# A two-layer graph attention kernel: products that end bank by bank, and rows spread by DMA rather than by transposes

## The chip, the cores and the metric

The kernel runs on one core of a Trainium2 chip. The metric is the device time of one launch in microseconds (us), the median over several runs. Everything is computed in 32-bit floats, except masks, which are stored as 16-bit floats.

## The reference

Two attention layers over a graph of 2708 nodes with 1024 features. `adj` is a 0/1 matrix of 2708 x 2708.

```python
# layer 0
h = jnp.maximum(_layernorm(x, axis=-1), 0.0)
f = h @ Wf + bf;  g = h @ Wg + bg
scores = jnp.where(adj > 0, jax.nn.relu(f @ g.T), -9e15)
x = x + jax.nn.softmax(scores, axis=1) @ (h @ W + bW)
# layer 1
h = jnp.maximum(_layernorm(x, axis=-1), 0.0)
hW = h @ W1;  f1 = hW @ a1;  f2 = hW @ a2
scores = jnp.where(adj > 0, jax.nn.leaky_relu(f1 + f2.T, negative_slope=0.2), -9e15)
x = x + jax.nn.relu(jax.nn.softmax(scores, axis=1) @ hW)
```

Two facts of it matter here. In layer 1 a score is a sum of something per row and something per column, so that a whole tile of scores is made from a column of numbers (one per partition) and a row of numbers spread over all partitions. In layer 0 the scores get a similar row, `r`.

## The kernel before

The kernel works in panels of columns of the transposed attention matrix: five panels (`NP` = 5), 576, 576, 532, 512 and 512 wide, each of two halves of `h` columns (288, 288, 266, 256, 256). The 2708 nodes along the other side are 20 tiles of 128, taken as ten pairs (`NQ` = 10), and two leftovers of 128 and 20 rows. All large products use seven products of half-size matrices in place of eight (M1 to M7, of Strassen's kind), with sums and differences on VectorE (DVE).

For each panel p, layer 0 runs `project_q`, `scores(p)`, the softmax, `aggregate(0, p)`, which multiplies the panel of weights with the features, and later `project(0, p)` by the weight matrix. Layer 1 has no score product: `weights1` makes the panel of weights on ScalarE (ACT) and DVE, and `aggregate(1, p)` and `project(1, p)` follow. The weights of panel p + 1 are made while panel p is multiplied.

**The aggregate.** `aggregate` hands its products in the order M1, M5, M2, M6, M3, M7, M4 to `accumulate` (L554 to L585). Each product accumulates into four PSUM banks (d = 0 to 3), named `gx`, `gy`, `gz` or `gv`. With `by_k` the loop runs over the ten pairs k outside and the four banks inside. After the last pair come the leftovers (`left_over`, L822 to L832: four matmuls of 128 rows, four of 20 rows, loaded as `hl`), and only then four evictions, one per bank, on ACT or DVE:

```python
if by_k:
    if m in more:
        more[m](ps)
    for d in range(NH):
        evict[m](d, ps[d])
    behind(rate)
```

M2 and M3 and M4 have such leftovers; those of M7 go apart into four banks `gw` in its middle (`into_m15`) and are added by DVE to a tile (`m15`, shown in the profile as `m<-gw`) before M7 is evicted. `prepare` and `then` are hooks after a product: after M3 the sums of the weights (`inverse_sums`: `sum_ps` by TensorE, a reciprocal on DVE), after M7 the scaling of results on GpSimd (`scale`).

**Rows out of columns.** A vector that lies as columns (128 partitions x up to 5) becomes a row on all partitions with `spread` (L229 to L240): a TensorE transpose of the column, broadcast, into a bank `sp_ps`, and copies of the bank into the tile, one for each four columns, in turn by DVE and ACT. So are made `rb` from `r` at the start of `scores(p)`, and in `weights1` the rows `ub` (from the columns `z`) and `vb1` (from `none`, called m in the code). The columns are made by DVE in `take_shifts(p + 1)`, the hook after M3 of layer 1's aggregate; the rows in `take_weights(p + 1)`, the hook after M7. A unit of weights P then is one ACT operation on `vb1`, one DVE operation on `ub`, one DVE addition of a mask tile (`maskl`), and an exponential on ACT.

**What sets the order.** TensorE, DVE, ACT and GpSimd each execute their queue in a fixed order, which a scheduler works out from the program and its dependencies when the kernel is built. SyncE (SP) issues loads in the order of the program (`load`); GpSimd issues the stores (`store`). Vector work that may be done at leisure is put in a list (`put`) and taken from it by `behind(us)`, which `accumulate` calls after every third pair and at a product's end.

Of the kernel before, what the change touches and what calls it, by code (L numbers as in the profile page):

```python
# [8 lines left out]
FP = mybir.dt.float32  # L9
# [9 lines left out]
P = 128  # L19
W = 512  # L20
# [37 lines left out]
def kernel(  # L58
# [19 lines left out]
    nc = InOrder(tc)  # L78
    N, D = x.shape
    NC = D // P  # L80
    NH = NC // 2
# [3 lines left out]
    NP = N // W  # L85
# [3 lines left out]
    width = [W + NM, W + NM, W + NY, W, W]  # L89
    base = [sum(width[:p]) for p in range(NP)]  # L90
    F = W // P
    MONO, TINY = F * NP, F * NP + 1
# [67 lines left out]
    md_d = dram.tile([P, 7, NH, W], FP, name="md_d")  # L160
    wt_d = [dram.tile([P, 4, NH, W], FP, name=f"wt{l}_d") for l in range(2)]
    mk_d = [dram.tile([P, NQ + 1, 2, width[p]], BF, name=f"mk_d{p}") for p in range(NP)]
    x1_d = [dram.tile([P if t < TINY else NY, D], FP, name=f"x1_d{t}") for t in range(NT)]

    ident = consts.tile([P, P], FP, name="ident")
# [31 lines left out]
    def behind(us, psum_free=False):  # L197
        credit[0] = min(credit[0] + us, 2 * us)
        while later and credit[0] > 0 and (psum_free or not later[0][3]) and (not later[0][4] or later[0][4]()):
            credit[0] -= one()  # L200

    def flush():
        while later:
            one()
# [24 lines left out]
    def spread(o, cols):  # L229

        at = 0
        for g in range(0, len(cols), 4):
            ps = bank("sp_ps")
            w = 0
            for cl in cols[g:g + 4]:
                n = cl.shape[0]
                nc.tensor.transpose(ps[:, w:w + n], cl.to_broadcast([n, P]), ident[:n, :n])
                w += n
            copy(o[:, at:at + w], ps[:, :w])
            at += w  # L240

    def add(o, a, b):
        nc.vector.tensor_tensor(o, a, b, OP.add)
# [4 lines left out]
    def columns_of(p, col):  # L248
        return [col[:n, i:i + 1] for i, (_, n) in enumerate(pieces[p])]
# [301 lines left out]
        picks.append(t)  # L551


    def accumulate(left, right, K, h, order, then, evict, name, prepare={}, rate=0.0, by_k=False, more={}, room=()):  # L554

        acc = {}
        at = {M1: "x", M2: "x", M5: "y", M3: "y", M6: "z", M7: "z", M4: "v" if by_k else "z"}
        for m in order:  # L560
            start = at[m] not in acc
            if start:
                acc[at[m]] = [bank(f"{name}{at[m]}{d}") for d in range(NH)]
            ps = [t[:, :h] for t in acc[at[m]]]
            for k, d in ([(k, d) for k in range(K) for d in range(NH)] if by_k else
                         [(k, d) for d in range(NH) for k in range(K)]):
                nc.tensor.matmul(ps[d], left(m, k, d), right(m, k), start=(start and k == 0),  # L567
                                 stop=(k == K - 1 and m not in more), skip_group_check=True)
                if by_k and d == NH - 1 and k % 3 == 2:
                    behind(rate)  # L570
                if by_k and d == NH - 1 and k == K // 2 and (m, k) in more:
                    more[m, k]()
                if not by_k and k == K - 1:
                    evict[m](d, ps[d])
                    behind(rate, m in room)
            if by_k:
                if m in more:
                    more[m](ps)
                for d in range(NH):
                    evict[m](d, ps[d])  # L580
                behind(rate)
            if m in prepare:
                prepare[m]()
            if m in then:
                then[m]()  # L585
# [202 lines left out]
    def aggregate(l, p, S, sm, then={}, rate=3.0):  # L788


        w = width[p]
        h = w // 2
        lo, hi = slice(0, h), slice(h, w)
        T1 = [slot("T1", (P, 2, HX)) for _ in range((NQ + 1) // 2)]
        t1 = lambda q: T1[q // 2][:, q % 2, :h]
        wa_ = lambda q: S[pairs[q][0]]
        wb_ = lambda q: S[pairs[q][1]]
        exps_until(NQ)
        for q in range(NQ):
            sub(t1(q), wa_(q)[:, hi], wa_(q)[:, lo])  # L800

        def second():
            exps_until(2 * NQ + 2 + LAG)
            for q in range(NQ):
                sub(wa_(q)[:, hi], wb_(q)[:, hi], wa_(q)[:, hi])
            for q in range(NQ):
                sub(wa_(q)[:, lo], wb_(q)[:, hi], t1(q))

        def fourth():
            for q in range(NQ):  # L810
                sub(wb_(q)[:, lo], wb_(q)[:, lo], wa_(q)[:, lo])

        hc = {}

        def left(m, q, d):
            i, j = group_of[q]
            if (m, i) not in hc:
                hc[m, i] = stream("hc", (P, 2, W))
                load(hc[m, i], hg_d[l][i][:, m])
            return hc[m, i][:, j, d * P:(d + 1) * P]  # L820

        def left_over(ps, e, s, start=False):  # L822


            two = stream("hl", (P, W + P))
            load(two, hgl_d[l][:, e])
            for d in range(NH):
                nc.tensor.matmul(ps[d], two[:, d * P:(d + 1) * P], S[MONO][:, s], start=start, stop=False,
                                 skip_group_check=True)
            for d in range(NH):  # L830
                g = slice(B32 * d, B32 * d + NY)
                nc.tensor.matmul(ps[d], two[g, W:], S[TINY][g, s], start=False, stop=True, skip_group_check=True)  # L832

        def into_m15():
            ps = [bank(f"gw{d}")[:, :h] for d in range(NH)]
            left_over(ps, 1, hi, True)
            for d in range(NH):
                add(get("m15", d), ps[d], get("m15", d))

        def right(m, q):  # L840
            if m == M5:
                return t1(q)
            s = wa_(q) if m in (M1, M6, M7) else wb_(q)
            return s[:, hi if m in (M3, M7) else lo]

        G = [None, None]
        tmp = {}
        part = lambda t, d: t[d // 2][:, d % 2, :h]

        def g(e, d, s):  # L850
            if G[0] is None:
                G[:] = both("gT")
            return G[e].rearrange("p (c i) -> p c i", c=NH)[:, d, s]

        def get(name, d):
            if name not in tmp:
                tmp[name] = in_pairs(name)
            return part(tmp[name], d)

        evict = {M1: lambda d, ps: nc.scalar.copy(get("m1", d), ps),  # L860
                 M5: lambda d, ps: add(get("m15", d), ps, get("m1", d)),
                 M2: lambda d, ps: nc.scalar.copy(g(0, d, lo), ps),
                 M6: lambda d, ps: add(get("u2", d), ps, get("m1", d)),
                 M3: lambda d, ps: add(g(0, d, hi), ps, get("u2", d)),
                 M7: lambda d, ps: (add(g(1, d, hi), ps, get("m15", d)), add(get("m1", d), ps, get("m1", d))),
                 M4: lambda d, ps: add(g(1, d, lo), ps, get("m1", d))}
        inverse = []
        of = lambda e, s: G[e].rearrange("p (c i) -> p c i", c=NH)[:, :, s]
        by = lambda s, k: inverse[0][:, s].rearrange("p (o i) -> p o i", o=1).to_broadcast([P, NH, k])

        def scale():
            for e, s, k in ((0, slice(0, w), w), (1, hi, h)):
                nc.gpsimd.tensor_tensor(of(e, s), of(e, s), by(s, k), OP.mult)  # L873

        accumulate(left, right, NQ, h, (M1, M5, M2, M6, M3, M7, M4), then, evict, "g",
                   {M5: second, M2: fourth, M3: lambda: inverse.append(inverse_sums(p, sm)), M7: scale}, rate=rate,
                   by_k=True, more={M2: lambda ps: left_over(ps, 0, lo), M3: lambda ps: left_over(ps, 0, hi),
                                    M4: lambda ps: left_over(ps, 1, lo), (M7, NQ // 2): into_m15})
        nc.vector.tensor_tensor(of(1, lo), of(1, lo), by(lo, h), OP.mult)
        return [t.rearrange("p (c i) -> p c i", c=NH) for t in G]  # L880
# [148 lines left out]
    def spread_wa():  # L1029
        for k in range(2):  # L1030
            spread(wab[k], [wa[:, k, c:c + 1] for c in range(NC)])
# [23 lines left out]
    def scores(p, B):  # L1055
# [3 lines left out]
        lo, hi = slice(0, h), slice(h, w)  # L1059
        fetch, convert, turn = makers[p]  # L1060
        rb = slot("rb")
        spread(rb, columns_of(p, r_[:, first_col[p]:]))
        acc = slot("acc")
        S = [None] * NT
        rates = (0.6, 1.0, 0.65, 0.65, 0.65)
# [36 lines left out]
        for q in range(NQ):  # L1102
            n = P
# [256 lines left out]
    for p in range(NP):  # L1360
# [17 lines left out]
        G[p] = aggregate(0, p, S, got["sm"], then)  # L1378
        if p == 0:
            flush()  # L1380
            spread_wa()
        if p < NP - 2:
            project(0, p, G.pop(p), finish0(p), {M1: lambda p=p: first_masks(p + 1, 0),
# [6 lines left out]
    def weights1(p, z, m, shift):  # L1390
# [2 lines left out]
        ub, vb1, sm = slot("ub"), slot("vb1"), slot("sm")  # L1393

        def spreads():
            spread(ub, columns_of(p, z))
            spread(vb1, columns_of(p, m))
        if p == 0:
# [67 lines left out]
    def take_shifts(p):  # L1466
        flush()
        got["zm"] = shifts1(p)

    def take_weights(p):  # L1470
        got["P"] = weights1(p, *got["zm"])
# [38 lines left out]
```

## Time and profile before

| | before |
|---|---|
| time, median of 3 | 3137.77 us (3136.57 to 3138.36) |
| profiled span | 3134.0 us |
| TensorE busy | 3046.8 us, 97%, 12712 instructions |
| DVE busy | 1827.0 us, 58% |
| ACT busy | 447.2 us, 14% |
| GpSimd busy | 464.3 us, 15% |
| granted TensorE clock, mean | 0.991 |
| DMA | 651.82 MB, 208 GB/s |

A 32-bit matmul is two instructions here, so the counts of TensorE are larger than the number of calls in the code. "Busy" counts the time in which an engine has an instruction under way; "waits" list the idle time of an engine by what ended it. The costliest groups of instructions are the matmuls of `aggregate` (L567), each product some 185 us in all, and those of the scores (L1077).

### The profile page before, as it was taken

To read this page: it belongs to the slowest core of one execution; us is meant where nothing else is said; L and a number is where in the kernel's file an instruction comes from. 1 tells how busy PE (TensorE), PEld (TensorE's weight loads), DVE (VectorE), ACT (ScalarE), POOL (GpSimd) and SP (SyncE) were. 2 spreads that over 40 slices of the span, in tenths; PEclk is the share of its full clock that TensorE was granted. 3 is DMA by queue.
4 is the path that set the end of the run, shared out by engine and by line. 5 is a ranking of instruction groups with operands and counts; after the bars stand their busy time and mean duration, and the time that the engine had idled before them with its cause. 6 is when DMAs were issued, how large, how long until landed. Compare 5 with 4: busy or idle time off the path is not lost.

```text
span 3134.0 us, 36230 instructions
## 1 busy us (share of the span) xinstructions
PE 3046.8 (97%) x12712; PEld 2261.3 (72%) x12712; DVE 1827.0 (58%) x3730; ACT 447.2 (14%) x788; POOL 464.3 (15%) x668
## 2 busy tenths in 40 slices
PE   8988999999999999999999999998999999999998
PEld 4566777667877588876888885865757758678684
DVE  5867686286732687327872478659483561745612
ACT  3321020000200102000020002103040130311200
POOL 2643002210002110023000101021010020120202
PEclk9989999999999999999999999998999999999999
DMA  6889838878446796477955678596665565565655
GB/s 219 307 284 280 258 122 311 231 228 253 147 134 159 220 258 205 147 175 240 294 167 154 169 220 243 192 300 234 194 186 168 160 197 162 164 197 171 216 163 190
DMA packets 379109, 651.82 MB, mean 208 GB/s; under 512 B 170848, under 2 KB 211328, under 8 KB 378928
## 3 DMA queue, kind: packets, MB, share of 16 engines
q1 hardware_dynamic: 335920, 525.38, 55.7%
q0 software_dynamic: 43008, 124.13, 11.9%
q8 instruction: 101, 1.65, 0.2%
q14 instruction: 80, 0.66, 0.1%
HBM read 536.68 MB, written 112.67 MB: 207 GB/s over the span
## 4 chain that ended last, share of the span: by engine, by line
PE 83%; DVE 5%; DMA 4%; issue 4%; POOL 2%; SPq 1%; ACT 0%; POOLq 0%; DVEq 0%; ACTq 0%
PE gy L567 12%; PE gz L567 12%; PE gx L567 11%; PE sz L1077 7%; PE gv L567 5%; PE pz L969 5%; PE sx L1077 5%; PE sy L1077 4%; PE px L969 4%; PE py L969 4%; PE qz L567 3%; PE qy L567 2%; PE qx L567 2%; SPq L139 1%; PE M_ps L483 1%
## 5 line engine op out<-in xcount | busy, mean ns | idle before, releaser
L1077 PE MATMUL sz<-B,As 128*128 128x288 f32 (+2 forms) x1200 | 292.7, 393 | 8.2 <-DVE st L45 7.5
L1077 PEld LDWEIGHTS sz<-B,As 128*128 128x128 f32 x1200 | 227.6, 190 | 58.3 <-DVE st L45 11.9
L873 POOL TENSOR_TENSOR gT<-gT,rr 128x2304 f32<-128x2304 f32 (+5 forms) x20 | 72.7, 3634 | 1101.0 <-DVE rr L45 998.6
L1077 PE MATMUL sx<-B,As 128*128 128x288 f32 (+2 forms) x800 | 201.5, 395 | 12.6 <-DMA As<-hs_d 11.7
L1077 PE MATMUL sy<-B,As 128*128 128x288 f32 (+2 forms) x800 | 199.0, 392 | 0.0
L567 PE MATMUL gz<-P,hc 128*128 128x288 f32 (+2 forms) x800 | 186.0, 393 | 2.3 <-ACT gT L45 2.3
L567 PE MATMUL gz<-Sa,hc 128*128 128x288 f32 (+2 forms) x800 | 186.0, 393 | 2.3 <-ACT gT L45 2.3
L567 PE MATMUL gx<-P,hc 128*128 128x288 f32 (+2 forms) x800 | 185.3, 393 | 0.1
L1077 PEld LDWEIGHTS sx<-B,As 128*128 128x128 f32 x800 | 152.3, 191 | 44.4 <-DMA As<-hs_d 12.2
L567 PE MATMUL gy<-T,hc 128*128 128x288 f32 (+2 forms) x800 | 184.2, 391 | 0.0
L567 PEld LDWEIGHTS gz<-Sa,hc 128*128 128x128 f32 x800 | 151.2, 190 | 36.0 <-ACT gT L45 4.4
L567 PEld LDWEIGHTS gz<-P,hc 128*128 128x128 f32 x800 | 150.9, 190 | 35.7 <-ACT gT L45 4.5
L567 PEld LDWEIGHTS gx<-P,hc 128*128 128x128 f32 x800 | 152.6, 191 | 32.7 <-issue 1.9
L567 PEld LDWEIGHTS gy<-T,hc 128*128 128x128 f32 x800 | 152.0, 190 | 30.5
L1077 PEld LDWEIGHTS sy<-B,As 128*128 128x128 f32 x800 | 151.7, 190 | 30.6 <-DVE st L45 0.3
L969 PE MATMUL pz<-w,ps 128*128 128x512 f32 x320 | 142.1, 594 | 0.8 <-DVE pt L45 0.8
L969 PE MATMUL py<-w,ps 128*128 128x512 f32 x320 | 142.1, 593 | 0.0
L969 PE MATMUL px<-w,gT 128*128 128x512 f32 x320 | 141.8, 595 | 0.0
L143 POOL DMA_DIRECT2D out_dram<-x_res x180 | 88.9, 500 | 265.3 <-DVE x_res L45 241.1
L45 DVE TENSOR_TENSOR gT<-gy,u 128x288 f32<-128x288 f32 (+2 forms) x40 | 14.8, 433 | 183.5 <-PE gy L832 183.5
L45 DVE TENSOR_TENSOR u<-gz,m 128x288 f32<-128x288 f32 (+2 forms) x40 | 17.6, 440 | 170.4 <-PE gz L567 169.9
L143 POOL DMA_DIRECT2D mk_d<-mask x55 | 35.9, 653 | 544.1 <-DVE mask L45 509.5
(318 smaller groups left out, 5089.8 us busy)
## 6 DMA issues: line engine op xcount, KB each, us to landing
hc<-hg_d SPq DMA_DIRECT2D x350, 512.0 KB, 3.9
As<-hs_d SPq DMA_DIRECT2D x150, 512.0 KB, 5.4
w<-wt_d SPq DMA_DIRECT2D x96, 512.0 KB, 5.2
w<-in_L_gnn_W_dram SPq DMA_DIRECT2D x72, 512.0 KB, 4.4
md<-md_d SPq DMA_DIRECT2D x56, 512.0 KB, 4.8
adj_i<-in_adj_dram SPq DMA_DIRECT2D x200, 128.0 KB, 5.0
hs_d<-hsT POOLq DMA_DIRECT2D x40, 512.0 KB, 5.0
hg_d<-g POOLq DMA_DIRECT2D x36, 512.0 KB, 5.1
```

Of the source, the lines that this page charges most:

```text
L45: i = f(*a, **k)
L139: tc.keep_in_program_order(nc.sync.dma_start(a, b))
L143: nc.gpsimd.dma_start(a, b)
L483: nc.tensor.matmul(ps, wfT[a][c // NH][:, c % NH, :], wgT[b][c], start=(c == 0), stop=(c == NC - 1))
L567: nc.tensor.matmul(ps[d], left(m, k, d), right(m, k), start=(start and k == 0), stop=(k == K - 1 and m not in more), skip_group_check=True)
L873: nc.gpsimd.tensor_tensor(of(e, s), of(e, s), by(s, k), OP.mult)
L969: nc.tensor.matmul(ps, left[i][m][:, k, :], w_[k], start=(start and k == 0), stop=(k == NH - 1), skip_group_check=True)
L1077: nc.tensor.matmul(ps[:n, :h], lefts[q][:, i % 2, c, :n], B[m][c // 2][:, c % 2, :h], start=(start and c == 0), stop=(c == NH - 1), skip_g ...
```

## The change

There are three parts. First, the products of the aggregate end bank by bank: eight of the ten pairs run as before, then the leftover products, and then for each bank the last two pairs, after which the bank is evicted at once. This lets the evictions overlap the product's own last matmuls. Second, the rows `r` of panels 1 to 4 are written to DRAM once by GpSimd and loaded back, spread over all partitions, by SyncE at the start of `scores(p)`. Third, the columns `z` and `none` of layer 1's panels 1 to 4 are written to DRAM by GpSimd in `take_shifts` as soon as they are ready, and loaded back as `ub` and `vb1` by two DMAs on GpSimd's queue. Both are meant to take the transposes and copies of `spread` from TensorE, DVE and ACT. Panel 0 keeps `spread` in both.

```diff
+    r_d = [dram.tile([1, WX], FP, name=f"r_d{p}") for p in range(NP)]
+    uv_d = [[dram.tile([1, WX], FP, name=f"uv{k}_d{p}") for k in range(2)] for p in range(NP)]
...
+    def columns_to_row(row, p, col):
+
+        k = len(pieces[p])
+        nc.gpsimd.dma_start(row[0:1, :W].rearrange("o (i p) -> p (o i)", p=P), col[:, :F])
+        if k > F:
+            n = pieces[p][F][1]
+            nc.gpsimd.dma_start(row[0:1, W:W + n].rearrange("o n -> n o"), col[:n, F:k])
+
+    def row_on_all(o, row, p, by=load):
+        by(o[:, :width[p]], row[0:1, :width[p]].to_broadcast([P, width[p]]))
...
+    TAIL = 2
...
-            for k, d in ([(k, d) for k in range(K) for d in range(NH)] if by_k else
-                         [(k, d) for d in range(NH) for k in range(K)]):
-                nc.tensor.matmul(ps[d], left(m, k, d), right(m, k), start=(start and k == 0),
-                                 stop=(k == K - 1 and m not in more), skip_group_check=True)
-                if by_k and d == NH - 1 and k % 3 == 2:
+            whole = K - TAIL
+            for k, d in ([(k, d) for k in range(whole) for d in range(NH)] + [(k, d) for d in range(NH) for k in range(whole, K)]
+                         if by_k else [(k, d) for d in range(NH) for k in range(K)]):
+                nc.tensor.matmul(ps[d], left(m, k, d), right(m, k), start=(start and k == 0), stop=(k == K - 1),
+                                 skip_group_check=True)
+                if by_k and d == NH - 1 and k < whole and (k % 3 == 2 or k == whole - 1):
                     behind(rate)
                 if by_k and d == NH - 1 and k == K // 2 and (m, k) in more:
                     more[m, k]()
-                if not by_k and k == K - 1:
+                if by_k and d == NH - 1 and k == whole - 1 and m in more:
+                    more[m](ps)
+                if k == K - 1:
                     evict[m](d, ps[d])
-                    behind(rate, m in room)
+                    if not by_k:
+                        behind(rate, m in room)
             if by_k:
-                if m in more:
-                    more[m](ps)
-                for d in range(NH):
-                    evict[m](d, ps[d])
                 behind(rate)
...
         rb = slot("rb")
-        spread(rb, columns_of(p, r_[:, first_col[p]:]))
+        if p == 0:
+            spread(rb, columns_of(p, r_[:, first_col[p]:]))
+        else:
+            row_on_all(rb, r_d[p], p)
...
             flush()
+            for s in range(1, NP):
+                columns_to_row(r_d[s], s, r_[:, first_col[s]:])
...
         def spreads():
+            if p > 0:
+                for o, row in zip((ub, vb1), uv_d[p]):
+                    row_on_all(o, row, p, nc.gpsimd.dma_start)
+                return
             spread(ub, columns_of(p, z))
             spread(vb1, columns_of(p, m))
...
     def take_shifts(p):
         flush()
         got["zm"] = shifts1(p)
+        for row, col in zip(uv_d[p], got["zm"]):
+            columns_to_row(row, p, col)
```

More of the change, by code (lines that the diff above doesn't have):

```diff
@@ L831, in left_over @@
                 g = slice(B32 * d, B32 * d + NY)
-                nc.tensor.matmul(ps[d], two[g, W:], S[TINY][g, s], start=False, stop=True, skip_group_check=True)
+                nc.tensor.matmul(ps[d], two[g, W:], S[TINY][g, s], start=False, stop=start, skip_group_check=True)
         def into_m15():
```

## The prediction

> **What bounds the kernel now.** I read the page's busy times first, then the chain of waits, then TensorE's waits by releaser, and last the timeline around those waits that the change touches.
>
> ```profile
> PE 3046.8 (97%) x12712; PEld 2261.3 (72%) x12712; DVE 1827.0 (58%) x3730; ACT 447.2 (14%) x788; POOL 464.3 (15%) x668
> PEclk9989999999999999999999999998999999999999
> ```
>
> TensorE (PE) is busy 97% of the span at nearly full clock; no other engine is near. Its chain share, 83%, says the same. So only two things pay: fewer TensorE instructions, or fewer gaps between them. DVE, ACT and GpSimd (POOL) time counts only where TensorE waits for it. The waits of TensorE in the kernel before (total us, times, longest):
>
> ```profile
> PE sx L1077 <- DMA As<-hs_d: 11.7, 1, 11.7
> PE sz L1077 <- DVE st L45: 7.5, 9, 1.4
> PE sum_ps L771 <- DVE gT L45: 5.1, 10, 0.5
> PE gz L567 <- ACT gT L45: 4.6, 10, 0.5
> PE sp_ps L237 <- DVE m L45: 3.8, 1, 3.8
> PE gx L567 <- DMA hc<-hg_d: 3.2, 1, 3.2
> PE gx L828 <- DMA hl<-hgl_d: 2.0, 1, 2.0
> ```
>
> The `sum_ps` and `gz` rows are ten waits each, one per panel and layer: in `aggregate`, after M2 the first matmul of M6, and after M3 the column sums, stand behind the evictions of a product that has just ended. The timeline of layer 1, panel 2 around the end of M3 and M7 (start us, us, engine and instruction, in brackets the idle time before it and its releaser):
>
> ```profile
> 2454.98 0.77 PE L832 MATMUL gy<-P,hl 20*128 20x288 f32 x8
> 2455.76 1.55 DVE L45 TENSOR_TENSOR gT<-gy,u 128x288 f32<-128x288 f32 x4 [21.56 <-PE gy L832]
> 2456.28 1.24 PE L771 MATMUL sum_ps<-sm,ones 128*128 128x288 f32 x4 [0.53 <-DVE gT L45]
> 2461.17 5.05 POOL L873 TENSOR_TENSOR gT<-gT,rr 128x2304 f32<-128x2304 f32 x1 [100.17 <-DVE rr L45]
> 2461.94 4.30 DVE L45 TENSOR_TENSOR z<-f,mcol 128x5 f32<-128x5 f32 x1
> 2466.97 0.16 DVE L45 SCALAR_TENSOR_TENSOR none<-f,m 128x5 f32<-128x5 f32 x1
> 2472.36 1.55 DVE L45 TENSOR_TENSOR m<-gw,m 128x288 f32<-128x288 f32 x4 [5.23 <-PE gw L832]
> ...
> 2480.14 0.76 PE L237 MATMUL sp_ps<-ident,z 128*128 128x128 f32 x5
> 2480.82 0.81 PE L237 MATMUL sp_ps<-ident,none 128*128 128x128 f32 x5
> 2481.56 4.63 PE L567 MATMUL gv<-P,hc 128*128 128x288 f32 x18
> 2481.81 0.68 DVE L45 COPY ub<-sp_ps 128x512 f32<-128x512 f32 x1
> 2482.41 0.68 DVE L45 COPY vb<-sp_ps 128x512 f32<-128x512 f32 x1
> 2484.64 1.99 ACT L45 ACTIVATE P<-vb,f2s 128x532 f32<-128x532 f32 x3
> 2485.40 0.77 DVE L45 SCALAR_TENSOR_TENSOR P<-ub,f,P 128x532 f32<-128x532 f32 x1 [2.32 <-ACT P L45]
> ```
>
> See three things. The product ends, DVE starts its four evictions, and only the first of them releases TensorE 0.53 us later. Between M7 and M4 TensorE does ten transposes, 1.42 us from the end of `gz` to the start of `gv`. And `z` and `none`, the columns that these turn into rows, are ready at 2467.1, 14.4 us before `gv` starts: that is the time that a path by DMA has.
>
> **What the Trainium skill says.** "TensorE: Matmul & The Clock Gate", Part 4: PE-mode transpose, gives about 275 ns for a transpose in one kernel's context; the median here is 273 ns, but they overlap, and ten cost 1.42 us. "DMA: Bandwidth & Descriptors", Anatomy of one DMA — SWDGE (gpsimd) path, fits 2.0 us plus bytes over 436 GB/s, mostly the wait for the receipt of the write; the same page, Rules for kernel authors, says that a non-contiguous last dimension becomes one descriptor per element. The transfers here take longer than the fit: 0.5 MB stores of `hg_d` land after 5.1 us, where the fit gives 3.2. "SBUF — State Buffer", SBUF: two separate sides, has DVE and GpSimd lock each other out of a shared port; the trace agrees: the 128x5 `z<-f,mcol` lasted 4.30 us beside a GpSimd scale, where its like `none` took 0.16.
>
> **Part 1: the last two pairs bank by bank.** No matmul is added. Leftover products move ahead of the last two pairs, and each of the four banks is evicted as it ends, two matmuls per bank earlier than the next. A matmul of 288 columns is two instructions; 80 of them took 19.40 us, 0.2425 each, so banks end 0.97 us apart, and three of the four are evicted before the product's end (an eviction takes 0.45). The first bank that the next product or the sums need has then been free for nearly 2 us. From the last small matmul to the next start I measured 0.87 us (`gz`) and 0.93 (`sum_ps`), against 0.33 where nothing is waited for: 0.54 and 0.60 too much at 288 columns, about 0.52 and 0.58 over all widths. M2 to M6 in nine aggregates: 9 x 0.53 = 4.8 us; M3 to sums in ten: 10 x 0.58 = 5.8. Together 10.6 us. The tenth, layer 0 panel 0, stands under a saturated DMA queue (the `hc` and `hl` rows above): its leftover load `hl` is now needed some 4 us earlier and ahead of the last `hc`, for which I take 1.5 us off (between 0 and 4), where the two waits together are 5.2 now.
>
> **Part 2: r by DMA in layer 0, panels 1 to 4.** 18 transposes and 4 + 4 copies go. In the timeline they hold TensorE for 0.7, 0.7, 0.45 and 0.5 us: 2.4 us. The rows are written once, right after panel 0's aggregate, some 100 us and more before they are read; the load stands on SyncE's queue ahead of the `adj_i` loads, waits for nothing recent and lands like a mask, 4.7 us. Nothing waits for it on TensorE: `rb` is first used by mask work in DVE's queue. Cost 0. The six small GpSimd issues (0.5 to 1.1 each) stand between stores with slack: 0.
>
> **Part 3: layer 1's rows by DMA, panels 1 to 4.** 36 transposes go: from `gz`'s end to `gv`'s start 1.51, 1.42, 0.88 and 0.87 us: 4.7 us. TensorE's count falls by 54 to 12658 over parts 2 and 3.
>
> The price is a new wait. The built order has, in DVE's queue of the changed kernel, the first `P<-ub` operations (two, and one or two mask adds) AHEAD of the four `m<-gw` evictions, and M4's first matmuls (`gv`) wait for those bank by bank, as `gv` takes the banks of `gw`. So `gv` now stands behind: `none` ready, GpSimd's element-wise writes of both columns, their receipt, the broadcast loads of `ub` and `vb1`, ACT's activation, and DVE's `P` work. Estimates: issue of a 128x4 write, 512 elements: the 128-run store costs 0.54 us and the 256-run one 0.73, so 0.19 per 128, thus 0.54 + 3 x 0.19 = 1.1 us; with the small rests (0.5 each, panels 1 and 2 only) the issues take 3.2 us. Landing, 3 to 5 us (`r<-r`, 64 elements, 2.9; `adj_i`, 512 runs, 5.0); overlapping the second column's issue, `ub` can be issued about 5 us after `none` and `vb1` 1.6 later; a 295 KB broadcast lands in 4.4 (the shortest `x_res<-bW`, such a broadcast): 11 us after `none`, 9.5 without rests. Then ACT 0.75, two `P<-ub` at 0.77, one mask add at 0.71 (two in panel 3) and the eviction 0.45: 3.6, 4.1 (panel 3), 3.4 us. Sum 14.6, 14.6, 13.6, 12.9. There is from `none` to `gv`, transposes taken off, 13.1, 13.0, 12.0 and 11.5. TensorE then waits 1.5 + 1.6 + 1.6 + 1.4, and with 0.4 us for two broadcasts under way at once, 6.5 us in all. From both sides: with every step at its shortest (landing 2.9, small rests overlapped) nothing is waited for; with landings of 5 for the write and 6.7 for the load, 14; if a write of 512 elements needs 5 us of descriptors (ten times the rate above), 40.
>
> While GpSimd waits for its writes, the second scale of `gT` (M7's half) stands behind it; the project's M2 needs that only after M4, 20 us on. DVE does `P` work earlier than before, which is work it has to do anyway, with M7's evictions behind: the banks `gz` aren't needed before the next product of that name. Both 0.
>
> **Sum.** −10.6 + 1.5 − 2.4 − 4.7 + 6.5 = −9.7: 3137.8 − 9.7 = 3128 us.
>
> **Rivals.** (a) The new wait is hidden: DMAs land within the 11 to 13 us. For it: the columns of a 128x5 tile are 2 KB, and the DMA share in layer 1 is the lowest of the kernel (0.59). Against: two landings in a row, neither of which is under 2.9 in the trace. Then −10.6 + 1.5 − 2.4 − 4.7 = −16.2, and without the 1.5 −17.7: 3120 to 3122 us. (b) The wait eats the gain: 3.5 us a panel rather than 1.6, with landings at the upper end: −16.2 + 14 = −2: 3136 us, within 0.2% (6.3 us). For it: broadcasts took 6.7 at the median. (c) Slower: the element-wise writes are built slowly or are held by DVE's port, 8 to 10 us a panel: −16 + 32 to 40: 3154 to 3162 us. For it: no row of the trace shows a write of 512 separate elements, and the chain has four of them in series with TensorE; against it: 256 runs cost only 0.19 us more than 128.
>
> **How the numbers follow.** Forecast (3123 to 3132) 0.40; (a) 0.23; (b) 0.22; (c) 0.15. The predicted time is 3128. The low end, 3117, lies a little under (a) for gaps that I may have undercounted; the high end, 3147, takes in all of (b) and the light half of (c), and leaves out some 0.1 above and less below. Faster by over 0.2% means under 3131.5: nearly all of the forecast and (a), 0.60. Slower means over 3144: (c), 0.15. Same: 0.25.
>
> **What would show it.** Part 1: the rows `gz` on ACT's `gT` and `sum_ps` on DVE's `gT` are gone from TensorE's waits, and evictions of M2 and M3 stand about 0.97 us apart. Part 2: the `rb` transposes are 5 rather than 23, and mask work starts no later. Part 3: a new row `gv` on DVE, four times, about 1.6 us each, with `P<-ub` on DVE and `P<-vb` on ACT behind a GpSimd DMA; the issues of `uv_d` at about 1.1 us. The prediction is wrong if that row is missing (a) or several microseconds each (b, c), or if the first aggregate's `hl` wait grows beyond 5 us.

## The result

The changed kernel takes 3188.23 us (3184.83 to 3188.47, four runs) against 3138.07 before: a ratio of 1.0158, with a 95% interval of 1.014 to 1.0175. It is 50 us slower, where 10 us faster was forecast.

TensorE's waits in the kernel after (total us, times, longest):

```profile
PE gv L583 <- DVE m L45: 45.6, 4, 11.9
PE sz L1095 <- DMA As<-hs_d: 9.3, 2, 5.0
PE qx L583 <- ACT m L45: 9.1, 1, 9.1
PE mx_ps L771 <- DVE mx L45: 8.3, 1, 8.3
PE sx L1095 <- DMA As<-hs_d: 7.3, 2, 6.0
PE sz L1095 <- DVE st L45: 6.9, 8, 1.4
...
PE gx L583 <- DMA hc<-hg_d: 5.2, 1, 5.2
```

The rows for `gz` on `gT` and for `sum_ps` on `gT` are gone, as meant. In their place stands the row that the prediction named, `gv` on DVE, but at 11.4 us a time and not 1.6. And the waits for `As` in layer 0's first scores have grown from 11.7 to 16.6 us.

The page has one more line to compare. TensorE is busy for longer, with 54 instructions fewer:

```profile
PE 3057.1 (96%) x12658; PEld 2268.5 (71%) x12658; DVE 1833.8 (58%) x3721; ACT 447.9 (14%) x779; POOL 481.4 (15%) x694
```

The timeline of the kernel after, layer 1's first aggregate, shows one of the four waits from end to end (start us, us, engine and instruction, idle time before it and its releaser):

```profile
2270.54 0.16 DVE L45 SCALAR_TENSOR_TENSOR none<-f,m 128x5 f32<-128x5 f32 x1
2270.92 0.78 POOL L247 DMA_DIRECT2D uv_d<-z  x1 [1.13 <-DVE none L45]
...
2280.88 0.57 POOL L253 DMA_DIRECT2D ub<-uv_d  x1 [7.31 <-DMA uv_d<-z]
2285.12 0.54 POOL L253 DMA_DIRECT2D vb<-uv_d  x1 [3.67 <-DMA uv_d<-none]
2291.77 2.11 ACT L45 ACTIVATE P<-vb,f2s 128x576 f32<-128x576 f32 x3 [21.55 <-DMA vb<-uv_d]
2292.58 1.54 DVE L45 SCALAR_TENSOR_TENSOR P<-ub,f,P 128x576 f32<-128x576 f32 x2 [21.89 <-ACT P L45]
2294.05 0.75 DVE L45 TENSOR_TENSOR P<-P,maskl 128x576 f32<-128x576 f32 x1
2294.71 1.54 DVE L45 TENSOR_TENSOR m<-gw,m 128x288 f32<-128x288 f32 x4
...
2295.22 17.54 PE L583 MATMUL gv<-P,hc 128*128 128x288 f32 x64 [11.20 <-DVE m L45]
```

Read the times from the top: the writes are issued at once and in 0.78 us, but `ub` can't be asked for until 2280.9 and `vb` until 2285.1; the second broadcast lands at 2291.8, 21.2 us after `none`. From there to `gv` it is 3.45 us of ACT, P work and an eviction. DVE had nothing else in the way: it sat idle 21.9 us with the eviction of `gw`, long ready, queued behind `P<-ub`.

What follows the wait costs as well. Windows of the same stage (us, busy time of TensorE, weight load, DVE, ACT, GpSimd; then the granted clock, DMA share, GB/s):

```profile
2292.00:2295.00 3.00, 0.00 (x0) 0.00 (x0) 2.42 (x4) 2.05 (x4) 0.00 (x0) 0.50 0.07 25
2295.00:2298.00 3.00, 2.78 (x6) 2.07 (x7) 3.00 (x8) 1.55 (x3) 0.00 (x0) 0.50 0.00 0
2298.00:2301.00 3.00, 3.00 (x12) 2.24 (x12) 3.00 (x6) 2.53 (x5) 0.00 (x0) 0.87 0.00 0
```

TensorE comes back at half clock: six matmul instructions in the first three microseconds, where windows of full clock further below have thirteen and more. A slower matmul is busy for longer; that is why "busy" grew.

**The ledger.** Laying the two traces against each other, start of each product against start of the same product, gives where the 50 us were lost, in us. The next product starts 0.42 us earlier before M6 and 0.48 before the sums; another 0.10 follows each time, since the first full matmul behind the 20-row ones takes 0.35 us instead of 0.24, and that one now lies ahead of the start that is compared. In layer 1 that 0.10 before M6 is given back at the product after it, four times; the last row of the table is net of it.

| step | predicted | measured |
|---|---|---|
| waits before M6, nine aggregates | −4.8 | −0.52 x 9 = −4.7 |
| waits before the sums, ten | −5.8 | −0.58 x 10 = −5.8 |
| first aggregate, up to M6 | +1.5 | +2.1 |
| r's transposes, layer 0 | −2.4 | −2.2 |
| first scores of layer 0 (`As`) | 0 | +9.2 |
| layer 1: wait of `gv` less transposes | +1.8 | +41.6 |
| matmuls after the four waits | 0 | +10.0 |

They sum to 50.2 us; the last product starts 50.1 us later. (The expectations below still reckon with 10.4 in the last row, 0.10 too much four times.)

Two rows hold more than waiting. In the first scores 4.3 us of the 9.2 are longer waits and about 4 are matmuls at half clock behind them; 0.5 was lost before they began. And in the first aggregate TensorE waits 5.2 us for transfers before and after alike, but in two pieces (3.2 and 2.0) before and in one after. Only behind the one piece was the clock down. Windows from there, after and then before:

```profile
518.00:521.00 3.00, 2.74 (x6) 2.03 (x7) 3.00 (x11) 0.00 (x0) 0.00 (x0) 0.50 1.02 416
...
516.00:519.00 3.00, 1.96 (x8) 1.44 (x8) 2.90 (x11) 0.00 (x0) 0.54 (x1) 1.00 1.03 420
```

### The profile page after: what moved, and what is told of

Its sections match the earlier page's. It is cut to its first block, busy times and chain, and to the rows that moved or that the text cites. A ratio compares the mean times of both kernels' runs of the same rounds, so it can differ in the third digit from the quotient of the medians.

```text
span 3183.1 us, 36143 instructions
## 1 busy us (share of the span) xinstructions
PE 3057.1 (96%) x12658; PEld 2268.5 (71%) x12658; DVE 1833.8 (58%) x3721; ACT 447.9 (14%) x779; POOL 481.4 (15%) x694
## 4 chain that ended last, share of the span: by engine, by line
PE 81%; DMA 6%; DVE 6%; issue 4%; SPq 1%; POOL 1%; ACT 0%; POOLq 0%; DVEq 0%; ACTq 0%
PE gy L583 12%; PE gx L583 11%; PE gz L583 9%; PE sz L1095 7%; PE pz L984 5%; PE gv L583 5%; PE sx L1095 4%; PE sy L1095 4%; PE py L984 3%; PE px L984 3%; PE qz L583 3%; PE M_ps L496 3%; PE qy L583 2%; PE qx L583 2%; SPq L139 1%
## 5 line engine op out<-in xcount | busy, mean ns | idle before, releaser
L583 PE MATMUL gv<-P,hc 128*128 128x288 f32 (+2 forms) x400 | 103.6, 423 | 45.6 <-DVE m L45 45.6
L583 PEld LDWEIGHTS gv<-P,hc 128*128 128x128 f32 x400 | 81.6, 207 | 67.1 <-DVE m L45 47.8
L45 DVE SCALAR_TENSOR_TENSOR P<-ub,f,P 128x512 f32<-128x512 f32 (+2 forms) x102 | 78.0, 771 | 85.6 <-ACT P L45 85.6
```

Of the source, the lines that this page charges most:

```text
L45: i = f(*a, **k)
```

## The experiments

The runs of the kernel before beside them had medians of 3139.4 to 3139.5 us; the expectations reckon from the 3138.07 of the result, so some 1.4 us of a miss is that.

**Each part alone.** Three kernels, each with one of the three parts of the diff and the rest as before.

> Part 1 alone: products end bank by bank, all rows by transposes as before. From the two traces, start of each product against start: the waits before M6 gave 0.42 us nine times, those before the column sums 0.48 us ten times, together 8.6 us, and the first aggregate lost 2.1 us before M6. Theory (nothing else of the change's loss belongs to part 1): 3138.1 - 8.6 + 2.1 = 3131.6 us, no wait of gv in layer 1, and the waits for As in layer 0's first scores as before (about 12 us in all). Rival (the 9.2 us lost in the first scores has nothing to do with r): about 3141 us.

Measured: 3128.24 us, ratio 0.9958 (0.9943 to 0.9973), the lowest median here, 3.4 us under the expectation. It had left out the 0.10 us behind each start, 1.9 us in all; the rest isn't accounted for. In the timeline of layer 1, panel 2, the evictions of M3 now stand apart, and TensorE goes straight on:

```profile
2450.55 0.46 DVE L45 TENSOR_TENSOR gT<-gy,u 128x288 f32<-128x288 f32 x1 [18.87 <-PE gy L583]
...
2451.51 0.46 DVE L45 TENSOR_TENSOR gT<-gy,u 128x288 f32<-128x288 f32 x1 [0.51 <-PE gy L583]
2452.49 0.46 DVE L45 TENSOR_TENSOR gT<-gy,u 128x288 f32<-128x288 f32 x1 [0.51 <-PE gy L583]
2453.25 1.13 PE L786 MATMUL sum_ps<-sm,ones 128*128 128x288 f32 x4
...
2453.45 0.46 DVE L45 TENSOR_TENSOR gT<-gy,u 128x288 f32<-128x288 f32 x1 [0.51 <-PE gy L583]
```

Banks end 0.97 us apart, and the sums start with no wait in brackets. `As` cost 13.5 us, about as before. Part 1 is a gain by itself.

> Part 2 alone: r of panels 1 to 4 by DMA. Theory (GpSimd's writes of 512 separate elements stand in the first scores, ahead of the stores of hs_d, and slow all transfers for some 10 us each): TensorE loses 9.2 us waiting for As in the first scores and saves 2.2 us of transposes: 3145 us. Rival (the 9.2 us are chance of that run): 3136 us.

Measured: 3146.19 us, ratio 1.0023 (1.0015 to 1.003). Part 2 alone makes the kernel slower. The timeline of its first scores, from the slowest of its eighteen runs:

```profile
288.07 0.76 POOL L247 DMA_DIRECT2D r_d<-r  x1 [3.41 <-DVE r L45]
...
301.97 3.88 PE L1093 MATMUL sx<-B,As 128*128 128x288 f32 x8 [11.21 <-DMA As<-hs_d]
```

The source has these writes after the first aggregate. But r is ready earlier, and the scheduler put them where it is ready: of the six, four before the first scores and two in them, where the score products wait for `As`, which waits for stores of `hs_d` on the same GpSimd queue. The same two stand there in the kernel after. DMA issues between 285 and 295 us, after and then before (KB, median us from issue to landing):

```profile
As<-hs_d SPq DMA_DIRECT2D x3, 512.0 KB, 13.6
hs_d<-hsT POOLq DMA_DIRECT2D x3, 512.0 KB, 14.4
...
As<-hs_d SPq DMA_DIRECT2D x3, 512.0 KB, 8.2
hs_d<-hsT POOLq DMA_DIRECT2D x3, 512.0 KB, 8.1
```

The stores and the loads that wait for them take longer by some 6 and 5 us.

> Part 3 alone: layer 1's rows by DMA. Theory (the wait of gv comes from this part alone): four waits of about 11 us, 41.6 us net of the transposes, and about 10.4 us of matmuls at a lower clock after them: 3190 us. Rival (the order on DVE that makes the wait is set by the bank by bank ends): no such wait, 3133 us.

Measured: 3197.35 us, ratio 1.0177 (1.0162 to 1.0192); `gv` waits 49.0 us in four. Part 3 makes the wait without any help from part 1.

**The order on DVE.** The whole change, with `gw`'s evictions held ahead of the P operations:

```diff
+            nc.hold = ("vector",) if l else ()
             for d in range(NH):
                 add(get("m15", d), ps[d], get("m15", d))
+            nc.hold = ()
...
+                    nc.hold = ("vector",)
                     nc.vector.scalar_tensor_tensor(s, ub[:n, :w], f[1][:n, t:t + 1], s, op0=OP.add, op1=OP.max)
+                    nc.hold = ()
```

> The whole change, but in layer 1 DVE's first P operations stand behind the evictions of gw, as in the kernel before; the DMAs stay as slow. Theory (it is the order on DVE that hands the DMAs' time to TensorE): the wait of gv and the slow matmuls behind it are gone, 3188.2 - 41.6 - 4.7 - 10.4 = 3131.5 us. Rival (the weights come too late wherever they stand): the wait moves to a later place, the next aggregate's first differences or the project, and the time stays above 3165 us.

Measured: 3139.89 us, ratio 1.0004 (0.9995 to 1.0014). The wait of `gv` is gone and with it the half clock behind it, so it is the order on DVE that handed the transfers' time to TensorE. But 8 us more than expected are left. The profiled run, the fastest of its twelve at 3135.2, has a new wait in layer 1:

```profile
PE px L986 <- ACT pt L45: 5.2, 3, 2.8
```

The weights P of panel 1 begin 7.0 us after `gv`, where it was 3.0 in the kernel before, and now crowd ACT and DVE in the projects that follow. Half clock follows there too: 0.62 and 0.81 in the two windows behind the wait of 2.8 us. The waits of all three panels and the slow matmuls behind them come to 7.7 us, about all of the 8. So the rival had a part of it: rows this late cost something even with the work on them behind the evictions.

**The write itself.** Part 1 alone, with one extra write of `z` for each panel, read by nobody:

```diff
+        if p == 1:
+            nc.gpsimd.dma_start(row[0:1, :W].rearrange("o (i p) -> p (o i)", p=P), z)
+        elif p == 2:
+            nc.gpsimd.dma_start(row[0:1, :W].rearrange("o (p i) -> p (o i)", p=P), z)
+        elif p == 3:
+            nc.gpsimd.dma_start(apart_d[:, 0:1].rearrange("(i p) o -> p (i o)", p=P), z)
+        else:
+            nc.gpsimd.dma_start(row[0:1, :P].rearrange("o p -> p o"), z[:, 0:1])
```

> Part 1 alone with one extra write of z per panel of layer 1 that nobody reads, in a form of its own: panel 1 as in the change (512 elements of 4 B, neighbours in the row come from 128 partitions), panel 2 the same tile in 128 runs of 16 B, panel 3 512 elements of 4 B spread 64 B apart, panel 4 one column, 128 elements of 4 B. Theory (the write is slow because of its many 4-byte pieces, not because GpSimd issues it): panel 1 lands after about 9 us and the loads of hc beside it stall; panel 2 in 3 to 5 us. If the number of pieces alone counts, panel 3 takes as long as panel 1 and panel 4 a quarter of it beyond a fixed 2 to 3 us; if it is that pieces share a stretch of memory, panel 3 is as quick as panel 2. Rival (GpSimd's queue or the receipt is slow in this stage): all four land after about 9 us. Time: 3128 to 3131 us, as nothing waits for these.

Measured (3128.71 us, one run): the view of DMA issues, one window for each panel in order (KB, us from issue to landing):

```profile
uv_d<-z POOLq DMA_DIRECT2D x1, 2.0 KB, 9.6
uv_d<-z POOLq DMA_DIRECT2D x1, 2.0 KB, 2.5
apart_d<-z POOLq DMA_DIRECT2D x1, 2.0 KB, 2.7
uv_d<-z POOLq DMA_DIRECT2D x1, 0.5 KB, 8.8
```

The number of pieces isn't what decides: 512 pieces set 64 B apart land in 2.7 us, and 128 pieces side by side need 8.8. What is slow is to put 4-byte pieces of different partitions next to one another in DRAM. Each form stood in one panel only, but other runs agree. Writes of 512 packed pieces in the kernel after are slow in all four panels (KB, median us):

```profile
uv_d<-z POOLq DMA_DIRECT2D x4, 2.0 KB, 10.1
uv_d<-none POOLq DMA_DIRECT2D x4, 2.0 KB, 11.3
```

And the runs of 16 B further below are quick in panels 2 to 4.

While a packed write lasts, the other transfers hardly move. Windows of the same run, the last number is GB/s; first beside the packed write of panel 1, then beside the runs of 16 B of panel 2:

```profile
2270.00:2273.00 3.00, 3.00 (x13) 2.37 (x13) 1.43 (x4) 0.00 (x0) 0.00 (x0) 1.00 0.31 18
2273.00:2276.00 3.00, 3.00 (x14) 2.32 (x13) 0.91 (x3) 0.00 (x0) 0.00 (x0) 1.00 0.40 10
...
2467.00:2470.00 3.00, 3.00 (x19) 1.86 (x18) 1.55 (x4) 0.00 (x0) 0.00 (x0) 1.00 0.80 186
2470.00:2473.00 3.00, 3.00 (x14) 2.37 (x13) 0.00 (x0) 0.00 (x0) 0.00 (x0) 1.00 0.45 164
```

From 2267 to 2276 us all transfers together moved 23, 18 and 10 GB/s in three windows, where part 1 alone, without the extra write, moved 76, 197 and 135. That fits how r's writes held up `As`. It is also a part of why the broadcasts behind such writes took 6.6 to 9.9 us in the kernel after, among the loads that had piled up; but without packed pieces they still took 4.9 to 6.4 in the next kernel.

**The change with that one thing mended.** The same instructions in the same order; the writes put runs of 16 B, which permutes the rows:

```diff
-        nc.gpsimd.dma_start(row[0:1, :W].rearrange("o (i p) -> p (o i)", p=P), col[:, :F])
+        nc.gpsimd.dma_start(row[0:1, :W].rearrange("o (p i) -> p (o i)", p=P), col[:, :F])
```

> The whole change with the same instructions in the same order on every engine; only the 128 x 4 writes of r, z and none put their elements as runs of 16 B (so the values stand in another order in the rows, and the output isn't the reference's). The rests of panels 1 and 2 (64 and 20 elements of 4 B) stay as they are. Theory (neighbouring 4-byte pieces from different partitions make the write slow, however few): in panels 3 and 4 the write lands in 2.5 us, the broadcasts in 4.5, and gv waits 0 to 2 us instead of 11.4 and 11.9; in panels 1 and 2 the rests keep the wait at 8 us or more. Saved: two waits of some 10.5 us, the slow matmuls behind them 2 x 2.8, and half of the 9.2 us in the first scores: about 3157 us. Rival (all that matters is that a DMA path of two landings stands in that place): four waits of 8 us or more, 3175 us or more.

Measured: 3139.97 us, ratio 1.0004 (0.9995 to 1.0013). The waits of `gv` in panels 1, 3 and 4, from the timeline:

```profile
2285.25 1.33 PE L583 MATMUL gv<-P,hc 128*128 128x288 f32 x2 [6.30 <-DVE m L45]
...
2688.00 2.29 PE L583 MATMUL gv<-P,hc 128*128 128x266 f32 x9 [1.75 <-DVE m L45]
...
2875.71 1.56 PE L583 MATMUL gv<-P,hc 128*128 128x256 f32 x6 [1.35 <-DVE m L45]
```

Without packed pieces, panels 3 and 4 wait 1.75 and 1.35 us; forecast were 1.6 and 1.4. That they meet is luck: the writes landed in 2.3 to 2.7 us, quicker than the 3 to 5 forecast, and the broadcasts in 6.0 to 6.4, slower than 4.4. Panel 1 still has its rest, 64 packed pieces that landed after 7.3 us, and waits 6.3. Half clock follows that wait as well, and the product of `gv` takes 2.7 us longer than in the kernel before:

```profile
2285.00:2288.00 3.00, 2.75 (x6) 2.04 (x7) 3.00 (x8) 1.56 (x3) 0.00 (x0) 0.50 0.00 0
```

Panel 2's rest, 20 pieces, landed in 2.8 us and left a wait of about 0.2; so few did little harm here, against what was expected. That, and the first scores back to 13.3 us for `As`, is why the time came out 17 us under the expectation. Runs of 16 B alone took 48 us off the changed kernel.

**Other ways to the same rows.** In the next, r keeps its element writes, but tied to the end of the first aggregate.

```diff
+            nc.vector.scalar_tensor_tensor(late[:n, c], G[0][1][:n, NH - 1, c], 0.0, r_[:n, c], op0=OP.mult, op1=OP.add)
...
+                columns_to_row(r_d[s], s, late[:, first_col[s]:])
```

> Part 1, and r by DMA with the same element writes, but tied to the end of the first aggregate (the columns are copied there, plus zero times its result), so that they can't run in the first scores. Theory (r lost time because the writes stood ahead of hs_d's stores there): the first scores wait for As about 12 us as before, and the time is part 1's 3128.2 - 2.2 = 3126 us, or a few us more if six such writes delay the first project's loads. Rival (such writes cost TensorE their 10 us wherever they stand): 3135 us or more.

Measured: 3136.41 us, ratio 0.999 (0.9983 to 0.9996), 8 us above part 1 alone. The first scores wait 11.9 us for `As`, so the placement was the reason there. But waits grew elsewhere: in panels 1 and 3 a later pass of `sx` waits for DVE's `sm<-sx,rb`, 2.4 and 2.9 us, where both panels together had 0.9 in the kernel before. In both places `sm<-sx,rb` stands on DVE behind work on a layer-norm tile, for which DVE itself waits 4.9 and 5.0 us, and half clock follows (0.55 and 0.54, where the kernel before had none). The two places start the next products 4.4 and 3.7 us later, about all of the 8. So the number was the rival's, 3135 or more. What made the layer-norm work late isn't shown. In panel 1 packed writes of r had taken 11 to 21 us to land, up to 637 us, some 30 us before the wait. In panel 3 no such write was near, and the broadcast of `rb` had landed 34 us before.

Two more kernels turn the columns into rows first, with one small transpose, and write runs of 512 B:

```diff
+        for j, c in enumerate(cols):
+            nc.tensor.transpose(ps[:F, j * P:(j + 1) * P], c[:, :F], ident)
+        nc.scalar.copy(t.rearrange("f j p -> f (j p)"), ps[:F, :2 * P])
...
+            nc.gpsimd.dma_start(row[0:1, :W].rearrange("o (i p) -> (o i) p", p=P), t[:, j, :])
```

> Part 1, and layer 1's rows by DMA, but the columns are turned first into rows by one transpose of 128 x 4 for each of z and none (after gw's products, in M7), so that DRAM is written in runs of 512 B; DVE's first P operations stand behind the evictions of gw. Theory: the writes land in 3 to 5 us, ub and vb1 some 10 us after none, no wait of gv; TensorE saves 4.7 us of transposes and pays about 0.4 a panel for the new ones: 3128.2 - 3.1 = 3125 us. Rival (the landings stay near 10 us, or P comes too late anyway): waits in the project as with gw first, 3131 us or more.

Measured: 3130.87 us, ratio 0.9972 (0.9962 to 0.9983). The writes land in 1.6 to 2.6 us, the broadcasts in 4.1 to 5.1, and `gv` doesn't wait. But the gain is small: the new transposes come with a wait (`row_ps` on DVE's `m`, 2.1 us in four), as their bank is one that `gw` has just used. This kernel and the next also hold `gw`'s evictions ahead of the P operations. Against part 1 alone layer 1 saves about 0.7 us in the profile; by their times the two can't be told apart, and the 3125 of the expectation was missed.

> As the kernel before it in this list, and r too by one transpose for all panels, runs of 512 B and broadcast loads. Theory: 2.2 us less: 3123 us. Rival (r by DMA loses time in the first scores for another reason than element writes): 3130 us or more.

Measured: 3131.68 us, ratio 0.9975 (0.9966 to 0.9984). With r as well nothing is gained, as the rival had it (3130 or more): the transposes are saved, but in panel 3's scores two products lose 0.6 and 0.8 us against part 1 alone, and smaller delays take the rest.

**The size of the tail.** Part 1 alone with `TAIL = 1`:

> Part 1 alone with the last pair, not the last two, bank by bank (TAIL = 1). The banks then end 0.49 us apart and the first is evicted 1.45 us before the product's end, still more than the 0.45 us of an eviction and the 0.08 to 0.13 us to its start, so the waits before M6 and before the sums stay away: the same gain of 8.6 us, and the leftover load is needed 2 us later in the first aggregate: 3127 us. Rival (half a microsecond is too tight for DVE, and TensorE waits a little again): 3130 us or more.

Measured: 3130.32 us, ratio 0.9974 (0.9963 to 0.9985). The waits stay away, and product by product the trace agrees with `TAIL = 2` to within 0.35 us from M3 of the first aggregate on. The median lies where the rival had put it, but the two can't be told apart by their times.

## Why the prediction was wrong

**Part 1 was right, its price by luck.** Both waits went, and the two sums came out at 4.7 and 5.8 us, 10.5 together where 10.6 were forecast. The first aggregate lost 2.1 us where 1.5 were forecast, but not for the reason given, the later use of `hl`: the waits are as long as before, and the loss is the half clock behind the one long wait.

**Part 3: the mechanism was right and one term mis-sized.** `gv` stands behind the whole chain as described, and its last link was well priced (3.45 us measured, 3.6 forecast in panel 1). The step that failed reads "Landing, 3 to 5 us". The writes of 512 pieces took 9.1 to 12.3 us, the broadcasts behind them 6.6 to 9.9 in place of 4.4. I took the landing from the nearest rows, `r<-r` (64 elements) and `adj_i` (512 runs); neither puts 4-byte pieces side by side in DRAM from many partitions. The 4.4 us were the shortest of the loads like it, `x_res<-bW`, whose median was 6.7. With the pieces in runs of 16 B the forecast waits of panels 3 and 4 came out to 0.15 us, by two errors that cancel. My question, how many descriptors, was the wrong one: issuing them took 0.78 us, less than my 1.1. "DMA: Bandwidth & Descriptors", Anatomy of one DMA — SWDGE (gpsimd) path, gives about 2.0 us for a small transfer in the Trainium skill; the write in runs of 16 B took 2.5, and the packed one 9.6, so the fixed price holds for the one and not for the other.

**A term was missing.** I counted a wait as its length. But behind an idle stretch of 11 us the clock was down, and each cost 1.8 to 2.9 us more, 10.0 in all. The skill says so in "TensorE: Matmul & The Clock Gate", Part 1: The HAM clock gate: after an idle window of about 3.4 us the clock is halved, and about as long a busy window restores it. The trace agrees: granted clock 0.50 in the first three microseconds, 0.87 in the next three. But half clock also followed waits shorter than that here, of 2.4, 2.8 and 2.9 us; behind 1.35, 1.75 and 1.9 us, and behind 3.2 in the first aggregate of the kernel before, it didn't.

**Part 2: the step "written once, right after panel 0's aggregate ... Cost 0" failed.** The source order isn't the order on GpSimd. The built order would have shown it; I had looked there for what waits, not for when. The first scores lost 9.2 us; with r's writes moved to the end of the first aggregate their waits for `As` were back to 11.9. (The copies that go are six, not the "4 + 4" of the prediction; nothing rests on it.) And `rb` isn't "first used by mask work": it is used by `sm<-sx,rb`, the evictions that a later pass of `sx` waits for.

**The rivals.** (c) had the right place and the wrong reason, slow building of descriptors or a port held by DVE. DVE was idle in those 21.9 us. Its 3154 to 3162 us fell short too: it had 8 to 10 us a panel where 11.4 came, and neither the half clock nor the first scores.

**What stays open** is what happens in the memory to packed 4-byte pieces. That they are written one after another where they share a stretch of it would fit the four forms and the 20 pieces that did no harm, but no run shows the mechanism, nor how long that stretch is.

## What to carry to other kernels

A column that becomes a row in DRAM should be written in runs, or be turned first: packed 4-byte pieces from 128 partitions took 9 us and more to land here, and held up other transfers meanwhile. Before a transfer is put in place of a cheap operation, read in the built order what stands behind its consumer, on every engine, and where the transfer itself is placed; the source tells neither. And a wait of TensorE should be priced with the slow matmuls behind it: here another 2.5 us for 11 us, and 2.7 for 6.3. Some waits of less than 3 us had them too.

## What the runs showed of the hardware

- A write of 512 4-byte pieces landed in 9.6 us packed and in 2.7 us set 64 B apart; 128 packed pieces took 8.8 us, and the same 2 KB in runs of 16 B 2.5.
- Beside a packed write of 512 pieces, all transfers together fell to 10 to 23 GB/s for nine microseconds, where the kernel without it moved 76 to 197.
- Behind waits of 2.4, 2.8, 2.9, 5.2, 6.3 and 11 us TensorE's granted clock was 0.50 to 0.62 in a window of three microseconds; behind 1.35 and 1.75 us it wasn't halved.
